# A planned state-space scan on one core: the skip term's matmuls moved to the middle of a half, an urgent copy out of PSUM, and a planner that places TensorE's matmuls one by one

## The chip, the core and the metric

The kernel runs on one core of a Trainium2 chip. The metric is the device time of one execution in microseconds. Before the change the median of three runs is 8321.25 us (8306.08 to 8322.18).

## The reference, cut to what matters

The network has two layers on an image batch `x` of 2 x 96 x 96 x 96. Layer 0 is a convolution block with a selective scan and a small quantized feed-forward net; layer 1 is an attention block with a feed-forward net of the same kind. The change lies in layer 0 (one helper that it touches, the feed-forward net, serves layer 1 too). Of layer 0 this much has to be seen:

```
x_s = grid_sample_bilinear(xin, pos)              # 192 channels, deformed by a learned offset
# the image is cut into 512 sequences of L = 36 pixels; 4 directions k, 192 channels d, 16 states n
x_dbl = einsum('bkdl,kcd->bkcl', xs4, x_proj_weight)      # dts, B, C
delta = softplus(dts @ dt_projs_weight + bias);  A = -exp(A_logs)
for each step t:
    h = h * exp(delta_t * A) + (delta_t * u_t) * B_t      # the scan
    y_t = sum over n of h * C_t
out_y = y + D * u                                          # the skip term
y = sum of the four directions; y = layernorm(y) * silu(z);  out = out_proj(y);  x = x + out
x = x + ffn(layernorm(x))
```

`D * u` is the skip term that the title speaks of. Since the four directions read the same pixels, the kernel adds the four D into one matrix and applies it once.

## The kernel before

Layer 0 works on 32 stripes of 6 image rows (576 pixels, `T`). A stripe has a **front** (`_l0_front`: normalize, project, 3x3 convolution, offsets, bilinear sampling into `xs0` and `xs1`, then B, C, delta and delta*u), a **scan** (`_l0_scan`) and a **back** (`_l0_back`: layer norm over `Y`, gate `zs`, output projection, feed-forward net). Front of stripe n+1, scan of stripe n and back of stripe n-1 run interleaved on the engines.

The scan of a stripe has two **halves** of 96 channels (`h`). Each half accumulates its output in one PSUM bank `y`, of which there is a single buffer. A half has four sections: `o` (row order or column order) times `kk` (forward, backward), each of four quarters of the states, each of two **units** `c` (288 pixels). So a half has 32 units, a stripe 64, and layer 0 has 2048. One unit u is this chain:

- TensorE, `spread` (L1115): B is spread over the partitions, into PSUM `bp` (two buffers, so it needs the scan of unit u-2 to be over);
- VectorE, `product` (L1119): `bp` becomes delta*u*B, then `scan` (L1136): the recurrence, into SBUF `h` (`P.nh` = 6 buffers, so it needs the fold of unit u-6);
- GpSimd, `times_c` (L1141): `h` times C, in place;
- TensorE, `states` (L1153), called the **fold** here: it sums over the states, and adds into `y`.

ScalarE makes the decays `exp(delta*A)` (`dA`, L1099) for two units at a time, two buffers.

At the start of a half, before its first fold, `direct` (L1040, L1042) writes D*u into `y` with six matmuls that also open the accumulation (`start=True`). After the last fold of a half, `out` (L1050, L1052) copies `y` on ScalarE to `Y`; only then can `direct` of the next half begin.

No engine's order is written by hand. All operations of layer 0 go to a planner (`_Plan`). It knows a cost for each operation, made up by hand or from the columns (`_cost`), a due time, the data dependencies and the buffers. `order()` takes in each step the operation that can start earliest; of those that could start at the same time it takes the earliest due. Operations of the scan have due times 60 units early on TensorE and ScalarE (`P.early`), so they win over front and back. An operation marked `first` does more: no other operation of its engine is placed that would end later than `HOLD` after the time at which the marked one can start. Before the change only `spread` is marked, and `out` has an ordinary due time, 33 units after the half's start. An operation may be a group: `run()` then issues several instructions at once, as `direct` does, or the two matmuls that sum over 192 channels in the front and the back.

The planned order is what the engines then follow, each strictly in its order, and each waiting for the data. In time that the plan leaves empty on TensorE, `keep` (L1197) writes matmuls into an unused corner of `y`; it does so only while `P.awake` names a half that is open. A half was opened by `direct`, and is closed by its last fold.

Of the kernel before, what the change touches and what calls it, by code (L numbers as in the profile page):

```python
# [26 lines left out]
C = 96  # L27
# [74 lines left out]
SAME = 0.06  # L102
LAG = {"pe": 0.5, "dve": 1.5, "act": 0.6, "pool": 1.0, "sp": 1.5}
SCAN_LAG = {"pe": 0.2, "dve": 0.3, "act": 0.2, "pool": 0.2, "sp": 1.5}
HOLD = 0.15
SPARE, SHARE, STEP = 0.15, 0.8, 0.15


# [379 lines left out]
def _l0_front(k, P, S, f, x, b, s, at):  # L488
# [157 lines left out]
    def offset(yx, c):  # L646
        po = ps("po")

        def run():
            rest = slice(64 * c, 64 * c + 64)  # L650
            nc.tensor.matmul(po.ap[:, :H2], k.w_off[:, 0, yx], t.ap[:, c], start=True, stop=False)
            nc.tensor.matmul(
                po.ap[:, :H2], k.w_off[rest, 1, yx], t.ap[rest, 2], start=False, stop=True)

        pe(2 * H2, run, ((t, c), (t, 2)), (po,), (fr,))
# [19 lines left out]
    def sample(half):  # L675
        n, X = PART[half], second if half else first
        v = lambda: xin.ap[:n, half, 1:8, 2 : HW + 2]
        fy, fx = lambda: fr.ap[:n, 0], lambda: fr.ap[:n, 1]
        d, tp, bt = (lambda u=u: u.ap[:n, half] for u in (dif, top, bot))
        D, TP, BT = (dif, half), (top, half), (bot, half)  # L680
        pool(672, lambda: tt(d(), xin.ap[:n, half, 1:8, 3 : HW + 3], v(), ALU.subtract), X, (D,))
        pool(T, lambda: tt(tp(), d()[:, 0:6], fx(), ALU.mult), (D, (fr, 1)), (TP,))
        pool(T, lambda: tt(tp(), tp(), v()[:, 0:6], ALU.add), X, (TP,))
        pool(T, lambda: tt(bt(), d()[:, 1:7], fx(), ALU.mult), (D, (fr, 1)), (BT,))
        pool(T, lambda: tt(bt(), bt(), v()[:, 1:7], ALU.add), X, (BT,))
        pool(T, lambda: tt(bt(), bt(), tp(), ALU.subtract), (TP,), (BT,))
        pool(T, lambda: tt(bt(), bt(), fy(), ALU.mult), ((fr, 0),), (BT,))

        def add(c):
            px = ps("px")  # L690
            rows = slice(3 * c, 3 * c + 3)

            def run():
                for j, u in enumerate((tp(), bt())):
                    nc.tensor.matmul(px.ap[:n, :H2], k.ident[:n, :n], u[:, rows, :],
                                     start=(j == 0), stop=(j == 1))

            pe(2 * H2, run, (TP, BT), (px,), (xs0, xs1))
            v = lambda: px.ap[:n, :H2].rearrange("p (i w j) -> p i w j", i=3, w=NW)
            act(H2, lambda: nc.scalar.copy(  # L700
                xs0.ap[:n, half].rearrange("p (w i j) -> p i w j", w=NW, i=WIN)[:, rows], v()),
                (px,), ((xs0, (half, c)),))
            act(H2, lambda: nc.scalar.copy(
                xs1.ap[:n, half].rearrange("p (w j i) -> p i w j", w=NW, j=WIN)[:, rows], v()),
                (px,), ((xs1, (half, c)),))

        for c in range(2):
            add(c)
# [9 lines left out]
    def order_of(o, xs):  # L718
# [4 lines left out]
        for c in range(2):  # L723


            def b_and_c(c=c):
                pb = ps("pb")
                cols = slice(c * H2, (c + 1) * H2)

                def run():  # L730
                    for half in range(2):
                        nc.tensor.matmul(
                            pb.ap[:, :H2],
                            k.w_bc[: PART[half], half, o].rearrange("p j k n -> p (j k n)"),
                            xs.ap[: PART[half], half, cols], start=(half == 0), stop=(half == 1))

                pe(2 * H2, run, (xs,), (pb,), (bt, rest))
# [12 lines left out]

            def deltas(c=c):
                pd = ps("pd")
                cols = slice(c * H2, (c + 1) * H2)

                def run():
                    for half in range(2):
                        nc.tensor.matmul(
                            pd.ap[:C, :H2], k.w_dl[: PART[half], half, o, :],
                            xs.ap[: PART[half], half, cols], start=(half == 0), stop=(half == 1))

                pe(2 * H2, run, (xs,), (pd,), (xd,))
# [112 lines left out]
def _plan_ffn(k, S, op, ps, temp, pool, bufs, ffn, x1, roomy=False):  # L874
# [50 lines left out]
    for c in range(2):  # L925
        def last(c=c):
            py = ps("fpy")

            def run():
                for m in range(NM):  # L930
                    nc.tensor.matmul(py.ap[:C, :H2], ffn.w2[:, m, :], h8.ap[:, m, cols(c)],
                                     start=(m == 0), stop=(m == NM - 1))

            op("pe", 3 * H2 // 2, run, (h8,), (py,), (y16,))
# [9 lines left out]
def _l0_back(k, P, S, f, ffn, res, dst, at):  # L944
# [14 lines left out]
    def both(w, src, name, r):  # L959

        out = ps(name)

        def run():
            for half in range(2):
                nc.tensor.matmul(out.ap[:C, :H2], w(half), src(half),
                                 start=(half == 0), stop=(half == 1))

        op("pe", 2 * H2, run, r, (out,))
        return out

    def centred(c):
# [25 lines left out]
    def project(c):  # L997
# [6 lines left out]
        def run():  # L1004
            nc.tensor.matmul(pp.ap[:C, :H2], k.ident[:C, :C], img(x1), start=True, stop=False)
            for n, (w, v) in enumerate(((k.w_outb, zs), (k.w_out, Y))):
                for h in range(2):
                    nc.tensor.matmul(pp.ap[:C, :H2], w[:, h, :], v.ap[:, h, cols(c)],
                                     start=False, stop=(n == 1 and h == 1))

        op("pe", 5 * H2, run, (Y, zs, (x1, c)), (pp,))
# [12 lines left out]
def _l0_scan(k, P, S, n, f, tau):  # L1024
# [4 lines left out]
    for h in range(2):  # L1029
# [3 lines left out]

        def direct(h=h, py=py):

            P.awake = py
            for b in range(NBL):
                g = NBL * h + b
                w, v = (u[: PART[g // 4]] for u in (k.w_D[:, g], f.xs0.ap[:, g // 4]))
                nc.tensor.matmul(py.ap[b * CB : b * CB + CB, :HEAD], w, v[:, :HEAD],  # L1040
                                 start=True, stop=False)
                nc.tensor.matmul(_tail(py, b), w, v[:, HEAD:], start=b == 0, stop=False)  # L1042

        S.op("pe", 1.4, direct, (f.xs0,), (py,), due=t0)
        for o in range(2):
            for kk in range(2):
                _l0_section(k, P, S, f, 64 * n + 32 * h, o, h, kk, py, t0 + (16 * o + 8 * kk) * tau, tau)

        def out(h=h, py=py):
# [1 line left out]
            for b in range(NBL):  # L1051
                nc.scalar.copy(f.Y.ap[b * CB : b * CB + CB, h, HEAD:], _tail(py, b))  # L1052

        S.op("act", 1.4, out, (py,), (f.Y,), due=t0 + 33 * tau)


HEAD = 14 * SEQ
# [8 lines left out]
def _l0_section(k, P, S, f, first, o, h, kk, py, at, tau):  # L1066
# [42 lines left out]
    def unit(u, i, c, cre, dA, t0):  # L1109
# [35 lines left out]
        S.op("pool", 1.7, times_c, (cre,), (ht,), due=t0 + (2.3 - P.early["pool"]) * tau, scan=True)  # L1145

        def states():
            end = o == 1 and kk == 1 and i == NQ - 1

            def part(dst, v, stop):  # L1150
                if o:
                    v = v.rearrange("p (w j i) -> p w i j", i=WIN, j=WIN)
                nc.tensor.matmul(dst, k.fold, v, start=False, stop=stop)  # L1153

            for blk in range(NBL):
                dst = py.ap[CB * blk : CB * blk + CB]
                n = HEAD - H2 if c else H2
                part(dst[:, c * H2 : c * H2 + n], ht.ap[:, blk, :n], end and c == 1)
            if c:
                for blk in range(NBL):  # L1160
                    part(_tail(py, blk), ht.ap[:, blk, n:], end and blk == NBL - 1)
            P.issued["pe", u] = latest()
            if end and c == 1:
                P.awake = None

        S.op("pe", 0.84, states, (ht,), (py,), due=t0 + (3.5 - P.early["pe"]) * tau, scan=True)

    for i in range(NQ):
        quarter(i)
# [880 lines left out]
```

## Time and profile before

| | us |
|---|---|
| median of three runs | 8321.25 |
| the profiled execution | 8317.46 |
| its span, first to last instruction | 8315.6 |
| layer 0's scans, first to last (146.7 to 6274.0) | 6127.3 |
| VectorE busy in that stretch | 5863.9 |
| TensorE, GpSimd, ScalarE busy in it | 5255.7, 5017.3, 4640.1 |

Busy time of an engine is the time in which at least one of its instructions ran. In the page's groups, each row gives line, engine, operation, tiles and shapes, then busy time, the mean duration of one, and the idle time of that engine just before, with what ended it. A float32 matmul shows as two records. PEld is the loading of weights, which overlaps the matmuls. The lines are those of the kernel before.

### The profile page before, as it was taken

How to read it: one execution, taken by the hardware profiler on the slowest of the kernel's cores; microseconds unless marked ns; L12 is line 12 of the kernel's file. 1: busy time of each engine (PE TensorE's matmuls, PEld its weight loads, DVE VectorE, ACT ScalarE, POOL GpSimd, SP SyncE). 2: the span in 40 equal slices, each digit the busy share in tenths (PEclk: the TensorE clock that was granted, in tenths of full speed). 3: DMA queues.
4: the chain of work that ended last, by engine and by line, in shares of the span. 5: the costliest groups of instructions: out<-in, count | busy, mean ns of one | idle time of the engine just before them, and what ended most of it. 6: DMA issues, size and time to landing. Idle time of an engine off the chain costs nothing. (4 is left out here: it accounts for less than half of the span.)

```text
span 8315.6 us, 123907 instructions
## 1 busy us (share of the span) xinstructions
PE 7287.6 (88%) x46090; PEld 3227.2 (39%) x46090; DVE 7623.0 (92%) x5404; ACT 6253.1 (75%) x10610; POOL 5184.1 (62%) x3835
## 2 busy tenths in 40 slices
PE   7888888888888888888888888888878999989998
PEld 3333333333333344333333333333334223542245
DVE  3999999999999999999999999999996998959988
ACT  5777777777777778787777777777746886678867
POOL 4888878788888888888878888888862000110001
PEclk9999999999999999999999999999999999989999
DMA  3554445444444445444444454544441000110001
GB/s 96 164 161 157 151 152 159 145 156 150 154 156 155 150 155 163 153 155 152 157 148 157 145 162 149 159 153 155 152 139 50 3 2 19 33 46 3 2 23 33
DMA packets 359849, 992.21 MB, mean 119 GB/s; under 512 B 69288, under 2 KB 71680, under 8 KB 359040
## 3 DMA queue, kind: packets, MB, share of 16 engines
q1 hardware_dynamic: 357440, 984.04, 37.7%
q8 instruction: 366, 6.00, 0.3%
q14 instruction: 251, 2.06, 0.1%
q10 hardware_dynamic: 1792, 0.12, 0.0%
HBM read 797.19 MB, written 139.25 MB: 113 GB/s over the span
## 5 line engine op out<-in xcount | busy, mean ns | idle before, releaser
L1141 POOL TENSOR_TENSOR h<-h,cre 128x864 f32<-128x864 f32 x2048 | 3486.0, 1714 | 1024.8 <-DVE h L1136 632.0
L1136 DVE TENSOR_TENSOR_SCAN h<-dA,bp 128x864 f32<-128x864 f32 x2048 | 3887.1, 1935 | 157.5 <-PE y L1153 145.9
L1099 ACT ACTIVATE dA<-dlr,A 128x576 f32<-128x576 f32 x3072 | 2156.9, 765 | 1019.6 <-DVE h L1136 914.7
L1119 DVE TENSOR_TENSOR bp<-dur,bp 128x864 f32<-128x864 f32 x2048 | 2062.7, 1045 | 155.3 <-DMA dur<-du_d 46.8
L1153 PE MATMUL y<-h,fold 128*32 128x288 f32 (+2 forms) x18432 | 1776.9, 437 | 103.4 <-POOL h L1141 98.5
L1115 PE MATMUL bp<-bt,selb 128*128 128x288 bf16 x2048 | 619.3, 302 | 690.1 <-DVE h L1136 679.2
L1512 ACT ACTIVATE pr<-sc 128x960 f32<-128x960 f32 (+1 forms) x1080 | 954.1, 937 | 199.7 <-PE sc L1508 178.3
L1153 PEld LDWEIGHTS y<-h,fold 128*32 128x32 f32 x18432 | 726.2, 114 | 746.3 <-POOL h L1141 396.3
L1592 DVE TENSOR_TENSOR sums<-sums,pr 128x3840 f32<-128x3840 f32 (+1 forms) x240 | 959.0, 3996 | 55.6 <-ACT pr L1512 33.1
L1684 POOL MEMSET vch<- 96x32 f32 x16 | 2.5, 154 | 1299.8 <-DVE dist L1546 1207.9
L1115 PEld LDWEIGHTS <-selb 128*128 128x128 bf16 x2048 | 197.4, 96 | 1348.3 <-DVE h L1136 1231.7
L1508 PE MATMUL sc<-qH,kH 32*128 32x480 f32 (+1 forms) x3240 | 627.0, 602 | 9.8 <-DMA q<-qH 5.3
L1197 PE MATMUL y<-selb,minus 128*32 128x288 bf16 x3205 | 598.1, 298 | 0.0
L1508 PE MATMUL sc<-q,kH 32*128 32x480 f32 (+1 forms) x1080 | 564.4, 602 | 0.0
L1574 PE MATMUL av<-pr,vT 128*32 128x480 f32 (+1 forms) x4320 | 533.0, 564 | 3.7 <-ACT av L1599 3.5
L1765 DVE SCALAR_TENSOR_TENSOR acc<-vch,lepe_w,acc 96x1152 f32<-96x1152 f32 x320 | 470.0, 1469 | 8.2 <-ACT vch L1700 0.4
L1508 PEld LDWEIGHTS sc<-qH,kH 32*128 32x128 f32 x3240 | 219.1, 184 | 418.8 <-issue 218.1
L1197 PEld LDWEIGHTS <-minus 128*32 128x32 bf16 x3205 | 272.4, 98 | 263.8 <-issue 192.3
L617 PE MATMUL pc<-xin,w_ca 128*128 128x288 f32 x1152 | 368.5, 423 | 0.1
L940 POOL TENSOR_TENSOR x<-x,fy 96x576 f32<-96x576 f32 x32 | 52.0, 1626 | 477.5 <-ACT fy L939 401.1
L797 PE MATMUL pt<-xd,w_dt 96*128 96x288 f32 x768 | 281.5, 454 | 4.3 <-ACT r L803 1.1
L816 POOL TENSOR_TENSOR e<-e,du 128x576 f32<-128x576 f32 x192 | 231.5, 1206 | 43.7 <-ACT du L812 43.6
(284 smaller groups left out, 10914.1 us busy)
## 6 DMA issues: line engine op xcount, KB each, us to landing
cre<-c_d SPq DMA_DIRECT2D x1024, 288.0 KB, 3.3
dur<-du_d SPq DMA_DIRECT2D x256, 864.0 KB, 5.5
dlr<-dl_d SPq DMA_DIRECT2D x256, 864.0 KB, 5.1
x<-xs SPq DMA_DIRECT2D x512, 72.0 KB, 2.8
du_d<-du SPq DMA_DIRECT2D x128, 288.0 KB, 2.9
dl_d<-dl SPq DMA_DIRECT2D x128, 288.0 KB, 4.0
du_d<-du SPq DMA_DIRECT2D x128, 144.0 KB, 2.5
dl_d<-dl SPq DMA_DIRECT2D x128, 144.0 KB, 3.0
```

The costliest lines, as they stand in the source:

```text
L1099: nc.scalar.activation(dA.ap[:, :, blk, :], dlr.ap[:, blk, :].rearrange("p (c n) -> p c n", c=2), AF.Exp, scale=k.A[:, i, kg, h, blk : blk ...
L1115: nc.tensor.matmul(bp.ap[:, :H2], k.selb[:, kk, i, :], f.bc[o].ap[:, toks], start=True, stop=True)
L1119: nc.vector.tensor_tensor(bp.ap[:, : NBL * H2].rearrange("p (b n) -> p b n", b=NBL)[:, ::-1], dur.ap[:, ::-1, toks], bp.ap[:, :H2].unsquee ...
L1136: nc.vector.tensor_tensor_scan(hv, dv, bv, 0.0, ALU.mult, ALU.add)
L1141: nc.gpsimd.tensor_tensor(ht.ap, ht.ap, cre.ap[:, toks].unsqueeze(1).to_broadcast([128, NBL, H2]), ALU.mult)
L1153: nc.tensor.matmul(dst, k.fold, v, start=False, stop=stop)
L1197: nc.tensor.matmul(P.awake.ap[NBL * CB :, T - HEAD + 2 * 72 : HEAD], k.minus[:, :CB], k.selb[:, 0].rearrange("p i m -> p (i m)")[:, : HEAD ...
L1508: nc.tensor.matmul(two[to // 2][:, to % 2, :n], kH[rows, k0 : k0 + 128], q, start=True, stop=True)
L1512: nc.scalar.activation(pr[:, 2 * i : 2 * i + 2, :n], two[i][:, :, :n], AF.Exp, scale=HD**-0.5)
L1574: nc.tensor.matmul((main if s < HEADS else other)[s * HD : (s + 1) * HD, :n], vT[:, blk, hd, :], pr[:, place(s, p), :n], start=at == 0, st ...
L1592: nc.vector.tensor_tensor(both, both, pr[:, :, :, :n], ALU.add)
L1765: S.op("dve", 1.43, lambda: nc.vector.scalar_tensor_tensor(acc.ap, src(), W.lw[:, t : t + 1], acc.ap, ALU.mult, ALU.add), (vch,), (acc,))
```

## The change

It has five parts.

1. `direct` moves from the start of a half to the start of the section o = 1, kk = 0 (unit 16 of 32), with its due time. It no longer opens the accumulation; the first folds of a half do (`start=True` for unit 0's and, for the tail columns, unit 1's).
2. `out` becomes an operation of the scan with a due time 60 units before the half's start, where it was 33 units after it.
3. `states` is marked `first`, as `spread` is; `HOLD` goes from 0.15 to 0.4.
4. Groups of matmuls in front, back and feed-forward net become single operations of the plan. What they compute, and in which order within a group, stays.
5. `P.awake` is set by the fold of unit 1 instead of by `direct`.

```
-HOLD = 0.15
+HOLD = 0.4
...
-            def run():
-                for j, u in enumerate((tp(), bt())):
-                    nc.tensor.matmul(px.ap[:n, :H2], k.ident[:n, :n], u[:, rows, :],
-                                     start=(j == 0), stop=(j == 1))
-
-            pe(2 * H2, run, (TP, BT), (px,), (xs0, xs1))
+            for j, u in enumerate((tp, bt)):
+                pe(H2, lambda j=j, u=u: nc.tensor.matmul(
+                    px.ap[:n, :H2], k.ident[:n, :n], u()[:, rows, :],
+                    start=(j == 0), stop=(j == 1)), (TP, BT), (px,), (xs0, xs1))
```

The same is done to the groups of `offset` (2 matmuls), `b_and_c` (2), `deltas` (2), `last` in the feed-forward net (3), `both` (2) and `project` in the back (5). Then, in `_l0_scan` and `_l0_section`:

```
         def direct(h=h, py=py):
 
-            P.awake = py
             for b in range(NBL):
                 ...
                 nc.tensor.matmul(py.ap[b * CB : b * CB + CB, :HEAD], w, v[:, :HEAD],
-                                 start=True, stop=False)
-                nc.tensor.matmul(_tail(py, b), w, v[:, HEAD:], start=b == 0, stop=False)
-
-        S.op("pe", 1.4, direct, (f.xs0,), (py,), due=t0)
+                                 start=False, stop=False)
+                nc.tensor.matmul(_tail(py, b), w, v[:, HEAD:], start=False, stop=False)
+
         for o in range(2):
             for kk in range(2):
+                if o and not kk:
+                    S.op("pe", 1.4, direct, (f.xs0,), (py,), due=t0 + 16 * tau)
                 _l0_section(...)
...
-        S.op("act", 1.4, out, (py,), (f.Y,), due=t0 + 33 * tau)
+        S.op("act", 1.4, out, (py,), (f.Y,), due=t0 - P.early["act"] * tau, scan=True)
...
         def states():
+            new = o == 0 and kk == 0 and i == 0
             end = o == 1 and kk == 1 and i == NQ - 1
             ...
-                part(dst[:, c * H2 : c * H2 + n], ht.ap[:, blk, :n], end and c == 1)
+                part(dst[:, c * H2 : c * H2 + n], ht.ap[:, blk, :n], end and c == 1, new and c == 0)
             ...
-            if end and c == 1:
-                P.awake = None
-
-        S.op("pe", 0.84, states, (ht,), (py,), due=t0 + (3.5 - P.early["pe"]) * tau, scan=True)
+            if c and (new or end):
+                P.awake = None if end else py
+
+        S.op("pe", 0.84, states, (ht,), (py,), due=t0 + (3.5 - P.early["pe"]) * tau,
+             scan=True, first=True)
```

More of the change, by code (lines that the diff above doesn't have):

```diff
@@ L647, in offset @@
         po = ps("po")
-        def run():
[L650 to L655, printed above, removed]
+        rest = slice(64 * c, 64 * c + 64)
+        pe(H2, lambda: nc.tensor.matmul(
+            po.ap[:, :H2], k.w_off[:, 0, yx], t.ap[:, c], start=True, stop=False),
+            ((t, c), (t, 2)), (po,), (fr,))
+        pe(H2, lambda: nc.tensor.matmul(
+            po.ap[:, :H2], k.w_off[rest, 1, yx], t.ap[rest, 2], start=False, stop=True),
+            ((t, 2),), (po,), (fr,))
         def share():
@@ L691, in add @@
             rows = slice(3 * c, 3 * c + 3)
-            def run():
-                for j, u in enumerate((tp(), bt())):
-                    nc.tensor.matmul(px.ap[:n, :H2], k.ident[:n, :n], u[:, rows, :],
-                                     start=(j == 0), stop=(j == 1))
-            pe(2 * H2, run, (TP, BT), (px,), (xs0, xs1))
+            for j, u in enumerate((tp, bt)):
+                pe(H2, lambda j=j, u=u: nc.tensor.matmul(
+                    px.ap[:n, :H2], k.ident[:n, :n], u()[:, rows, :],
+                    start=(j == 0), stop=(j == 1)), (TP, BT), (px,), (xs0, xs1))
             v = lambda: px.ap[:n, :H2].rearrange("p (i w j) -> p i w j", i=3, w=NW)
@@ L728, in b_and_c @@
                 cols = slice(c * H2, (c + 1) * H2)
[L730 to L737, printed above, removed]
+                for half in range(2):
+                    pe(H2, lambda half=half: nc.tensor.matmul(
+                        pb.ap[:, :H2],
+                        k.w_bc[: PART[half], half, o].rearrange("p j k n -> p (j k n)"),
+                        xs.ap[: PART[half], half, cols], start=(half == 0), stop=(half == 1)),
+                        (xs,), (pb,), (bt, rest))
                 def split():
@@ L753, in deltas @@
                 cols = slice(c * H2, (c + 1) * H2)
[L755 to L761, printed above, removed]
+                for half in range(2):
+                    pe(H2, lambda half=half: nc.tensor.matmul(
+                        pd.ap[:C, :H2], k.w_dl[: PART[half], half, o, :],
+                        xs.ap[: PART[half], half, cols], start=(half == 0), stop=(half == 1)),
+                        (xs,), (pd,), (xd,))
                 act(H2, lambda: nc.scalar.copy(xd.ap[:, cols], pd.ap[:C, :H2]), (pd,), ((xd, c),))
@@ L927, in last @@
             py = ps("fpy")
[L929 to L934, printed above, removed]
+            for m in range(NM):
+                op("pe", H2 // 2, lambda m=m: nc.tensor.matmul(
+                    py.ap[:C, :H2], ffn.w2[:, m, :], h8.ap[:, m, cols(c)],
+                    start=(m == 0), stop=(m == NM - 1)), (h8,), (py,), (y16,))
             op("act", H2, lambda: nc.scalar.copy(y16.ap[:, cols(c)], py.ap[:C, :H2]),
@@ L961, in both @@
         out = ps(name)
[L963 to L968, printed above, removed]
+        for half in range(2):
+            op("pe", H2, lambda half=half: nc.tensor.matmul(
+                out.ap[:C, :H2], w(half), src(half), start=(half == 0), stop=(half == 1)),
+                r, (out,))
         return out
@@ L1002, in project @@
             "p i (w j) -> p w i j", j=WIN)
[L1004 to L1011, printed above, removed]
+        op("pe", H2, lambda: nc.tensor.matmul(
+            pp.ap[:C, :H2], k.ident[:C, :C], img(x1), start=True, stop=False), (Y, zs, (x1, c)), (pp,))
+        for n, (w, v) in enumerate(((k.w_outb, zs), (k.w_out, Y))):
+            for h in range(2):
+                op("pe", H2, lambda n=n, w=w, v=v, h=h: nc.tensor.matmul(
+                    pp.ap[:C, :H2], w[:, h, :], v.ap[:, h, cols(c)],
+                    start=False, stop=(n == 1 and h == 1)), (v,), (pp,))
         op("act", H2, lambda: nc.scalar.copy(
@@ L1147, in states, with part @@
         def states():
+            new = o == 0 and kk == 0 and i == 0
             end = o == 1 and kk == 1 and i == NQ - 1
-            def part(dst, v, stop):
+            def part(dst, v, stop, start):
                 if o:
                     v = v.rearrange("p (w j i) -> p w i j", i=WIN, j=WIN)
-                nc.tensor.matmul(dst, k.fold, v, start=False, stop=stop)
+                nc.tensor.matmul(dst, k.fold, v, start=start, stop=stop)
             for blk in range(NBL):
@@ L1157, in states @@
                 n = HEAD - H2 if c else H2
-                part(dst[:, c * H2 : c * H2 + n], ht.ap[:, blk, :n], end and c == 1)
+                part(dst[:, c * H2 : c * H2 + n], ht.ap[:, blk, :n], end and c == 1, new and c == 0)
             if c:
                 for blk in range(NBL):
-                    part(_tail(py, blk), ht.ap[:, blk, n:], end and blk == NBL - 1)
+                    part(_tail(py, blk), ht.ap[:, blk, n:], end and blk == NBL - 1, new and blk == 0)
             P.issued["pe", u] = latest()
-            if end and c == 1:
-                P.awake = None
-        S.op("pe", 0.84, states, (ht,), (py,), due=t0 + (3.5 - P.early["pe"]) * tau, scan=True)
+            if c and (new or end):
+                P.awake = None if end else py
+        S.op("pe", 0.84, states, (ht,), (py,), due=t0 + (3.5 - P.early["pe"]) * tau,
+             scan=True, first=True)
     for i in range(NQ):
```

## Prediction, made before the changed kernel was run

> **What bounds the kernel now.** I read the busy time of layer 0's stretch first (the table by windows), then who VectorE waits for in it, then the timeline of each engine around the longest wait. From the windows:
>
> ```profile
> 146.70:6274.00 6127.30, 5255.73 (x33729) 2389.65 (x33728) 5863.89 (x4278) 4640.07 (x8079) 5017.30 (x3606) 0.95 0.48 153
> ```
>
> Columns are the length, then busy time of TensorE, its weight loads, VectorE, ScalarE, GpSimd. VectorE is busy 5863.9 of 6127.3 us; 263.4 us are idle. Two groups of the page make nearly all of its work, and GpSimd's largest shows the next resource:
>
> ```profile
> L1141 POOL TENSOR_TENSOR h<-h,cre 128x864 f32<-128x864 f32 x2048 | 3486.0, 1714 | 1024.8 <-DVE h L1136 632.0
> L1136 DVE TENSOR_TENSOR_SCAN h<-dA,bp 128x864 f32<-128x864 f32 x2048 | 3887.1, 1935 | 157.5 <-PE y L1153 145.9
> L1119 DVE TENSOR_TENSOR bp<-dur,bp 128x864 f32<-128x864 f32 x2048 | 2062.7, 1045 | 155.3 <-DMA dur<-du_d 46.8
> ```
>
> Per unit VectorE needs 3887.1/2048 = 1.90 us for the scan and 2062.7/2048 = 1.01 for the product. The change touches neither, so it can win or lose only idle time: at most 263 us here. The waits of VectorE in that stretch (us in all, times, longest):
>
> ```profile
> DVE h L1136 <- PE y L1153: 145.9, 46, 9.8
> DVE bp L1119 <- PE bp L1115: 32.8, 52, 1.4
> DVE bp L1119 <- PE y L1153: 30.3, 23, 1.6
> ```
>
> The first is the scan waiting for a fold, that is for one of the six `h` buffers. Counting scans up to each of its 46 waits: 16 stand before the same scan, that of unit 6 of the second half of a stripe, and hold 121.3 us. Thirteen of these last 8.1 to 9.8 us. One, on VectorE, TensorE and ScalarE:
>
> ```profile
> 821.77 1.06 DVE L1119 TENSOR_TENSOR bp<-dur,bp 128x864 f32<-128x864 f32 x1
> 831.93 3.80 DVE L1136 TENSOR_TENSOR_SCAN h<-dA,bp 128x864 f32<-128x864 f32 x2 [9.10 <-PE y L1153]
> ```
>
> ```profile
> 821.43 0.30 PE L1115 MATMUL bp<-bt,selb 128*128 128x288 bf16 x1 [0.44 <-DVE h L1136]
> 821.57 1.15 PE L579 MATMUL pz<-xn,in_proj 96*96 96x288 f32 x4
> 825.62 1.21 PE L579 MATMUL pz<-xn,in_proj 96*96 96x288 f32 x4 [2.90 <-ACT zs L582]
> 827.05 1.05 PE L1040 MATMUL y<-xs,w_D 128*32 128x504 f32 x1 [0.22 <-ACT Y L1052]
> ...
> 829.71 1.06 PE L1040 MATMUL y<-xs,w_D 64*32 64x504 f32 x2
> 830.70 1.54 PE L1153 MATMUL y<-h,fold 128*32 128x288 f32 x15
> ```
>
> ```profile
> 823.86 1.28 ACT L582 ACT_TABLE_LOAD   x1
> 825.15 0.71 ACT L582 ACTIVATE zs<-pz 96x288 f32<-96x288 f32 x2
> 825.75 0.57 ACT L1050 COPY Y<-y 96x504 f32<-96x504 f32 x1
> 826.34 0.66 ACT L1052 COPY Y<-y 32x72 f32<-32x72 f32 x3
> ```
>
> The chain: `out` stands on ScalarE behind a table load and two gates; `direct` stands on TensorE behind two `pz` matmuls that need those gates; the first fold of the new half stands behind `direct`, which takes 3.7 us here (827.05 to 830.77). VectorE has filled all six buffers and waits.
>
> **The skill.** *TensorE: Matmul & The Clock Gate*, "Step-by-step: what each phase is for": "The MATMULs themselves stay in program order". The trace agrees: a fold with its data ready waits 2.90 us behind a `pz`. The same page, "What's actually happening": after an idle window of about 3.4 us the array runs at half clock. `direct` takes 1.06 to 2.0 us at the boundaries that don't stall and 3.0 to 3.7 at the thirteen that do; the gap before it is 2.90 us, a little under that window, so the clock may be why, but this trace doesn't prove it. *ScalarE: Activation LUTs*, "What ACT_TABLE_LOAD costs": about 1283 ns a load; the trace has 1283 for each.
>
> **The change, part by part.** I compared the built order of both kernels, instruction by instruction on each engine; it holds no times.
>
> *Moving `direct`, urgent `out` (parts 1, 2).* At 13 boundaries of the old order `out` stands behind the decays of units u+8, and the first fold behind the spread of u+7, four `pz` and `direct`: the thirteen long waits. In the new order this is left at one boundary of 63 (stripe 4). Elsewhere `out` stands behind the decays of u+2 or u+4, eight times of u+6. The start of scan u+6 lies 15.3 us (median of the trace) after the end of scan u. Decays of u+4 can start when scan u+1 is over, 2.9 us into that; then at most 2.5 us of other work, decays 2.1, `out` 1.23, fold 0.7: done by 9.5 of 15.3. With u+6: start at 8.7, then 2.1 + 1.8 + 1.23 + 0.7 = 14.5, still inside. So **-121.3 us, +8.7** for the one left (a mean long wait). Between 0 and 130 is possible.
>
> *`direct` in the middle.* Its six matmuls now stand behind the spread of unit 17 to 22, with one to four folds behind them, since all folds from unit 16 on write the same `y`. Worst case, behind the spread of unit 22: spread 0.3 + direct 2.0 + fold 0.7 = 3.0 us, while VectorE has a scan (1.9) and two products (2.0) before it needs unit 16's buffer. The last fold of such a pile delays the next spread; the new order has the product of the other unit 5.8 us later there. Taken 0; if `direct` took the cold 3.7, 1 us a half, 64 us.
>
> *Folds `first`, `HOLD`, single matmuls (3, 4).* A fold standing behind the spread of unit u+6 or u+7 is one that leaves VectorE hardly any time. There are 161 + 59 = 220 in the old order and 83 + 34 = 117 in the new, 47% fewer. The waits for folds outside the boundary are 145.9 - 121.3 + 30.3 = 54.9 us; 47% of that is **-26 us** (0 to -55). HOLD 0.4 lets another matmul run 0.25 longer past the moment a spread is due. The second product of a pair has about 0.5 us to spare (first product 1.0, less the spread's 0.3 and the hand-over), so most of that is hidden; I add **+10 us** to the 32.8 (bounds 0 and 250, see the rivals).
>
> *GpSimd.* Nothing is added, but the order moves. Front and back put runs of tensor operations of 1.21 us between two `times_c`. Runs of twelve or more: 14 in the old order (all of twelve), 30 in the new (20 of twelve, 10 of thirteen). A run of twelve (14.5 to 14.9) with `times_c` before and after (2 x 1.7) and a fold with its hand-over (0.9) ends 19.2 us after scan u; the buffer of u+1 is needed at 2.9 + 15.3 = 18.2. That is 1.0 us each, and 2.3 for thirteen. Old 14 x 1.0, new 20 x 1.0 + 10 x 2.3 = 43: **+29 us** (0 to 112, the latter 3.5 us in each of 32 stripes).
>
> *ScalarE.* The gates are planned in more pieces: 22 more loads of their table and 22 back, 44 x 1.283 = 56 us. Cover: ScalarE is busy 4640 of 6127, and decays may come 5.6 us late (two scans and four products, 7.7, less their 2.1) while a load, a gate and a load back take 3.0. Taken 0 (0 to +56).
>
> *The rest.* `keep` goes from 3205 to 3528 matmuls, 323 x 0.14 us in gaps of TensorE's plan: 0, hidden as TensorE is busy 86%. DMAs: as many as before, SP's order shifts with the plan; waits for `dur` were one, at the start: 0. In layer 1 the feed-forward's three last matmuls are planned singly; SP and GpSimd keep their order there, the others shift locally: 0, +-8.
>
> Sum: -121.3 + 8.7 - 26 + 10 + 29 = -99.6 us. The profiled execution took 8317.5 us by its own time, 0.05% under the median of 8321.25, so I need no correction: 8317.5 - 99.6 = **8218 us**.
>
> **Rivals.** *GpSimd takes it back* (0.2): the stall gave GpSimd its time to catch up; without it the runs cost 1.8 to 3.5 us in every stripe, 58 to 112 instead of 29: 8247 to 8300, I take 8280. For it: GpSimd's lag already grows to 15 us behind the scan at unit 7. Against: it is busy 82% and idle 2.6 us at the long wait.
> *Spreads come late* (0.09), which ends slower: were HOLD's 0.25 us not hidden, each of the 1010 pairs of products would pay it: +250, 8317.5 - 121 + 9 - 26 + 29 + 250 = 8458. It decides once spreads end over 0.6 us after the scan that frees them. Against: a 288-column float32 matmul takes 0.48 us back to back where the planner charges 0.58, so the real engine runs ahead of its plan; and VectorE waited for a spread only 52 times in 2048.
> *The wait changes its name* (0.06): `out` is still late, since ScalarE's order changes little in time or table loads come ahead of it: 8317.
> The forecast has 0.65.
>
> **Numbers.** A measurement of this kernel can tell about 0.2% (17 us) from no change. The forecast's own range, with 0 to -55 for folds and half the bounds of the others, is 8160 to 8270; the GpSimd case reaches to 8300. Range 8150 to 8300. Faster by over 0.2%: 0.84 (forecast and nearly all of the GpSimd case), within: 0.07, slower: 0.09.
>
> **What would show it.** After: the wait of the scan (L1125) for `y` L1143 drops from 145.9 to below 50 us, no wait of 8 us but one; VectorE's idle time in layer 0 is near 165 us; D's matmuls take 1 to 2 us. GpSimd's case shows as scans of units 9 to 14 waiting for folds that waited for L1130; late spreads as `bp` L1108 waiting for L1104 with far over 33 us. I am wrong if long waits at the boundary are gone and the time isn't.

## The result, and the profile after

The changed kernel takes 8276.36 us (median of five, 8270.01 to 8282.34) against 8321.25 (8304.28 to 8322.18). The ratio of the means is 0.9954, with a 95% interval from 0.994 to 0.9969. It is faster, by 45 us by the medians and 38 by the means, where 103 were forecast. The profiled execution took 8276.3 us, 41.2 less than the one before.

The table by windows for the new layer 0, from the start of its first scan to the end of its last (length, then busy TensorE, weight loads, VectorE, ScalarE, GpSimd, then the granted clock):

```profile
149.40:6226.90 6077.50, 5297.01 (x34106) 2420.16 (x34105) 5896.18 (x4278) 4695.24 (x8118) 5018.97 (x3605) 0.96 0.49 154
```

VectorE's idle time is 181.3 us, but its busy time has grown by 32.3. The same three groups of the page:

```profile
L1130 POOL TENSOR_TENSOR h<-h,cre 128x864 f32<-128x864 f32 x2048 | 3475.2, 1713 | 957.4 <-DVE h L1125 639.7
L1125 DVE TENSOR_TENSOR_SCAN h<-dA,bp 128x864 f32<-128x864 f32 x2048 | 3900.6, 1939 | 51.2 <-PE y L1143 30.6
...
L1108 DVE TENSOR_TENSOR bp<-dur,bp 128x864 f32<-128x864 f32 x2048 | 2082.2, 1048 | 187.9 <-PE bp L1104 81.4
```

The scan's idle time fell from 157.5 to 51.2 us; the product's rose from 155.3 to 187.9, and its main releaser is now the spread. VectorE's waits in that stretch (us in all, times, longest):

```profile
DVE bp L1108 <- PE bp L1104: 81.4, 106, 2.6
DVE h L1125 <- PE y L1143: 30.6, 26, 4.7
DVE bp L1108 <- POOL h L1130: 27.8, 40, 1.9
```

Scans waited for folds for 145.9 us and now do for 30.6. Products waited for spreads for 32.8 and now do for 81.4.

For all comparisons I measured each kernel from the start of its first scan to the end of its last (before: 146.7 to 6269.9), and sorted VectorE's waits of 0.15 us or more by what ended them. "Boundary" is the scan of unit 6 of a half waiting for a fold. "Just behind `times_c`" is a wait for a fold that ended at most 1.3 us after its own `times_c`, so that GpSimd and not TensorE's queue held it up; the other folds waited for ended 1.8 us or more after theirs.

| us | before | after | difference | forecast |
|---|---|---|---|---|
| stretch | 6123.2 | 6077.6 | -45.6 | -99.6 |
| VectorE busy | 5863.9 | 5896.3 | +32.4 | 0 |
| boundary waits (number) | 121.4 (16) | 4.7 (1) | -116.7 | -112.6 |
| other waits for folds | 54.8 | 28.7 | -26.1 | -26 |
| of these, just behind `times_c` | 9.1 | 23.1 | +14.0 | |
| waits for `times_c` | 17.0 | 28.3 | +11.3 | +29 |
| waits for spreads (number) | 32.8 (52) | 81.4 (106) | +48.6 | +10 |
| all other idle time | 33.3 | 38.2 | +4.9 | 0 |

Around the stretch, the start came 2.7 us later and layer 1 took 1.9 us more. So three questions stand: why VectorE is busier, why spreads come late, and which part of the change ended the boundary waits.

### The profile page after: what moved, and what is told of

It is laid out like the page before. It is cut to its first block, busy times and chain, and to the rows that moved or that the text cites. A ratio compares the mean times of both kernels' runs of the same rounds, so it can differ in the third digit from the quotient of the medians.

```text
span 8274.5 us, 124621 instructions
## 1 busy us (share of the span) xinstructions
PE 7337.5 (89%) x46413; PEld 3261.5 (39%) x46413; DVE 7653.1 (92%) x5404; ACT 6308.6 (76%) x10654; POOL 5188.3 (63%) x3835
## 5 line engine op out<-in xcount | busy, mean ns | idle before, releaser
L1125 DVE TENSOR_TENSOR_SCAN h<-dA,bp 128x864 f32<-128x864 f32 x2048 | 3900.6, 1939 | 51.2 <-PE y L1143 30.6
L1108 DVE TENSOR_TENSOR bp<-dur,bp 128x864 f32<-128x864 f32 x2048 | 2082.2, 1048 | 187.9 <-PE bp L1104 81.4
L1188 PEld LDWEIGHTS <-minus 128*32 128x32 bf16 x3528 | 298.0, 98 | 225.6 <-issue 131.2
L810 POOL TENSOR_TENSOR e<-e,du 128x576 f32<-128x576 f32 x192 | 231.1, 1204 | 60.0 <-ACT du L806 59.7
```

What stands on the lines that cost most here:

```text
L1108: nc.vector.tensor_tensor(bp.ap[:, : NBL * H2].rearrange("p (b n) -> p b n", b=NBL)[:, ::-1], dur.ap[:, ::-1, toks], bp.ap[:, :H2].unsquee ...
L1125: nc.vector.tensor_tensor_scan(hv, dv, bv, 0.0, ALU.mult, ALU.add)
L1188: nc.tensor.matmul(P.awake.ap[NBL * CB :, T - HEAD + 2 * 72 : HEAD], k.minus[:, :CB], k.selb[:, 0].rearrange("p i m -> p (i m)")[:, : HEAD ...
```

## The experiments

Each kernel was timed beside the kernel before. In the table, the columns from "busy" on are microseconds in the stretch of the profiled execution: VectorE's busy and idle time, its boundary waits, its waits for spreads, and the time in which the trace gives TensorE's clock as 0.5 ("half clock"). "Pairs" is the edit of E4.

| kernel | us | ratio (95%) | busy | idle | boundary | spread | half clock |
|---|---|---|---|---|---|---|---|
| before | 8321.25 | | 5863.9 | 259.3 | 121.4 | 32.8 | 597 |
| after | 8276.36 | 0.9954 (0.994-0.9969) | 5896.3 | 181.3 | 4.7 | 81.4 | 430 |
| E1 parts 1, 2, 5 | 8267.99 | 0.9942 (0.9929-0.9954) | 5866.1 | 201.4 | 40.3 | 40.0 | 290 |
| E2 part 4 | 8262.2 | 0.994 (0.9927-0.9953) | 5873.0 | 197.2 | 44.1 | 52.3 | 570 |
| E3 part 3 | 8240.15 | 0.9914 (0.9899-0.9929) | 5882.2 | 171.4 | 82.6 | 58.3 | 365 |
| E4 after + pairs | 8199.41 | 0.9859 (0.9845-0.9873) | 5861.2 | 132.2 | 0 | 127.2 | 304 |
| E5 before + pairs | 8096.92 | 0.9737 (0.9724-0.975) | 5852.7 | 48.1 | 0 | 13.5 | 116 |
| E6 E5, HOLD 0.4 | 8154.82 | 0.9804 (0.9791-0.9818) | 5858.3 | 105.6 | 0 | 95.7 | 375 |
| E7 all dependent | 8497.3 | 1.0219 (1.0204-1.0235) | 6061.0 | 230.9 | 79.3* | 31.4 | 341 |
| E8 after, HOLD 0.15 | 8466.02 | 1.018 (1.0166-1.0194) | 5877.4 | 402.8 | 237.8 | 78.5 | 911 |
| E9 before, D's cost | 8284.07 | 0.9954 (0.9939-0.9969) | 5870.0 | 231.1 | 71.7 | 63.6 | 700 |
| E10 after, HOLD 0.41 | 8359.03 | 1.0053 (1.0037-1.007) | 5895.0 | 242.0 | 101.6 | 21.2 | 99 |
| E11 E4, folds not first | 8197.76 | 0.9847 (0.983-0.9864) | 5867.2 | 139.8 | 0 | 60.9 | 440 |
| E12 E1 + pairs | 8184.36 | 0.983 (0.9815-0.9846) | 5862.5 | 129.9 | 0 | 102.0 | 403 |
| E13 after, more keep | 8244.32 | 0.99 (0.9882-0.9918) | 5894.4 | 156.7 | 5.6 | 53.0 | 270 |
| E14 after, no keep | 8415.74 | 1.0106 (1.0085-1.0127) | 5909.4 | 317.1 | 4.7 | 165.7 | 1896 |
| E15 E6, more keep | 8107.33 | 0.9741 (0.9723-0.9758) | 5857.7 | 56.2 | 0 | 46.3 | 181 |
| E16 E12, more keep | 8172.03 | 0.9815 (0.9796-0.9835) | 5859.6 | 106.0 | 0 | 57.2 | 232 |
| E17 E5, more keep | 8095.57 | 0.9726 (0.971-0.9742) | 5852.4 | 46.4 | 0 | 15.4 | 72 |

*In E7 product and scan are issued as one, and this wait shows at the product of unit 6 instead of its scan: 25 waits, twelve of them of 6.0 us.

### The parts alone: E1, E2, E3

E1 is the kernel before with `direct` in the middle, `out` urgent and `P.awake` set by the fold. E2 is the kernel before with part 4's single matmuls. E3 is this:

```
-HOLD = 0.15
+HOLD = 0.4
...
-        S.op("pe", 0.84, states, ..., scan=True)
+        S.op("pe", 0.84, states, ..., scan=True, first=True)
```

> The kernel before with parts 1, 2 and 5 alone: D in the middle of a half, the copy of y urgent; HOLD stays 0.15, folds are not first, groups stay groups. In its built order no product stands directly before its own scan on VectorE, 213 folds stand behind the spread of u+6 or u+7 (220 before), the copy stands behind the decays of u+8 at 10 boundaries (13 before), and GpSimd has 25 runs of twelve or thirteen operations. Theory (the gain is the end of the chain copy, D, fold; the loss of the whole change comes from late spreads and from products directly before their scans, which parts 3 and 4 bring): a boundary wait is left at those 10 but without D's 3.7 us, some 5 us each, so -121 + 50; spread waits stay near 33 us; GpSimd's runs +25: about 8270. Rival (the place of the copy alone decides, D is nothing): 10 x 9 us stay, 8310.

> The kernel before with part 4 alone: single matmuls in the plan; D opens the half as before, the copy has its old due time, HOLD 0.15. In its built order the copy stands behind the decays of u+8 at one boundary of 63 only, 162 folds stand behind the spread of u+6 or u+7, no product stands directly before its own scan. Theory that the thirteen waits are an accident of the planned order (any part that reshuffles it ends them): -121 + 9, folds -15, spread waits near 33: about 8195, faster than the whole change. Rival (D and the copy must be moved to end the waits): 8310 to 8320.

> The kernel before with part 3 alone: folds first, HOLD 0.4. Its built order has 188 products directly before their own scan, 56 folds behind the spread of u+6 or u+7, the copy behind the decays of u+8 at 10 boundaries with D behind it. Theory (part 3 brings late spreads and dependent pairs): spread waits near 80 us (+48), 188 pairs at 0.125 us +24, folds -25, boundary waits 10 x 9 instead of 121: about 8335. Rival (part 3 only helps, late spreads come from single matmuls): spread waits stay near 33 and the time is 8260 to 8280.

E1 came out as forecast; E2, forecast at 8195, and E3, at 8335, did not. Each part alone is as good as all together or better: 0.9942, 0.994 and 0.9914 against 0.9954. If gains added up, the three would give 2.0%; together they give 0.46%. E1 has 15 boundary waits left, nine of 3.5 to 7.3 us, so moving D and urging the copy does not end them by itself. E2, which moves neither, cuts them from 121.4 to 44.1 us. VectorE's busy time grows by 2.2 us in E1, 9.1 in E2 and 18.3 in E3: most of the extra busy time comes with part 3, some with part 4.

### VectorE's busy time: E4, E7

In VectorE's built order of the kernel before, no scan stands directly behind its own product; P(u), P(u+1), S(u), S(u+1) is the usual run. In the order after, 233 scans do; in E3's, 188. E4 forbids it, with one more dependency in the planner ("pairs"): the scan of an even unit comes after the product of the odd one.

```
-        S.op("dve", 0.96, product, ...)
-        S.op("dve", 1.87, scan, ...)
+        prod = S.op("dve", 0.96, product, ...)
+        sc = S.op("dve", 1.87, scan, ...)
+        if c:
+            P.even.deps.add(prod)
+        P.even = sc
```

E7 does the opposite to the kernel after: product and scan are one operation of the plan, so that all scans follow their own product.

```
+        def both():
+            product()
+            scan()
+        S.op("dve", 2.83, both, (dur, dA), (bp, ht), due=t0 - P.early["dve"] * tau, scan=True)
```

> The changed kernel with one line more in the plan: the scan of an even unit depends on the product of the odd unit after it, so products and scans come in pairs. In its built order no product stands directly before its own scan (233 in the changed kernel), 5 folds stand behind the spread of u+6 or u+7 (117), GpSimd has one run of twelve (30), the copy never stands later than behind the decays of u+4. Theory (a product directly before its own scan loses the overlap of two instructions, 0.125 us): VectorE's busy time falls by 29 us, waits for folds go to near 5 us (-25), spread waits stay near 80: about 8220. Rival (the pairs only turn the loss into waits for the odd unit's spread): busy time falls and spread waits grow by as much, 8265 to 8280.

> The changed kernel with product and scan of a unit as one operation of the plan, so that all 2048 products (233 in the changed kernel) stand directly before their own scans. The next spread has a whole product and scan, 2.9 us, to be done. Theory (a product directly before its own scan costs the overlap of two neighbours, 0.125 us): VectorE's busy time falls by little or none while its gaps under 0.15 us and lost overlaps add 1815 x 0.125 = 227 us, spread waits go to under 10 us (-75), boundary waits come back at 12 places (+50): about 8475. Rival (it costs nothing; the busy time of the changed kernel rose for another reason): about 8250.

E7 on VectorE's timeline (start, duration, instruction):

```profile
2999.43 1.04 DVE L1108 TENSOR_TENSOR bp<-dur,bp 128x864 f32<-128x864 f32 x1
3000.51 1.95 DVE L1124 TENSOR_TENSOR_SCAN h<-dA,bp 128x864 f32<-128x864 f32 x1
3002.38 1.04 DVE L1108 TENSOR_TENSOR bp<-dur,bp 128x864 f32<-128x864 f32 x1
```

The product ends at 3000.47 and its scan starts at 3000.51: a gap. That scan ends at 3002.46, but the next product, which doesn't need it, has started at 3002.38: an overlap of 80 ns. A unit takes 2.95 us. With pairs, on the timeline of E5 (below), both changes overlap:

```profile
3002.08 3.79 DVE L1136 TENSOR_TENSOR_SCAN h<-dA,bp 128x864 f32<-128x864 f32 x2
3005.78 2.00 DVE L1119 TENSOR_TENSOR bp<-dur,bp 128x864 f32<-128x864 f32 x2
3007.69 1.95 DVE L1136 TENSOR_TENSOR_SCAN h<-dA,bp 128x864 f32<-128x864 f32 x1
```

Two units take 3007.69 - 3002.08 = 5.61 us, 2.81 each. Over E7, against E4, the price of one dependent pair is (6061.0 - 5861.2 + 75.3)/2047 = 0.134 us, where 75.3 is the sum of E7's gaps under 0.15 us, nearly all of them the 34 ns behind a product (1.1 in E4). For the 233 pairs of the change that makes an estimated 31 us: 8.6 of gaps (idle time) and about 23 of the 32.4 of busy time. Lost overlap by itself is 19.1 us there (the sum of all durations less the busy time falls from 342.1 to 323.0); the other 13.3 are longer durations, of which only a part is the pairs': E2, without a dependent pair, has 9.6 us of them, and their cause is open. E4, with none, takes 77 us less than the kernel after; its stretch is 84 us shorter, 35 of it busy time and 49 idle. Pairs also leave no boundary wait and 3.0 us of waits for folds; but spreads come late for 127.2 us. E7's boundary waits came back at the twelve places forecast.

### The pairs without the change: E5, E6

E5 is the kernel before with the pairs alone. E6 is E5 with HOLD 0.4 instead of 0.15.

> The kernel before, with none of the change, and the line that makes products and scans come in pairs (the scan of an even unit depends on the product of the odd one). HOLD 0.15. Its built order has no product directly before its own scan, as before, but the plan comes out otherwise: the copy never stands later than behind the decays of u+4 (13 times behind u+8 before), 64 folds stand behind the spread of u+6 or u+7 (220), GpSimd has one run of twelve (14). Theory (the thirteen waits are an accident of the plan; late spreads come with HOLD 0.4): no boundary waits though D opens the half and the copy isn't urgent, folds 10, spreads 35 to 50: idle near 75 us instead of 259, 8130 to 8145. Rival (spread waits show as soon as the other waits go, whatever HOLD is): spread waits over 100 us, 8190 to 8210.

> As the kernel before with pairs, and HOLD 0.4 instead of 0.15; folds are not first, groups stay groups. In its built order 3 folds stand behind the spread of u+6 or u+7, the copy stands behind the decays of u+2 but for one boundary. Nothing but spreads is left to wait for. Theory (HOLD is what makes spreads late): spread waits 80 to 130 us against those of the kernel with HOLD 0.15, time 8190. Rival (folds marked first make spreads late): spread waits as with HOLD 0.15, time 8130.

E5's waits of VectorE in layer 0:

```profile
DVE bp L1119 <- issue: 19.0, 27, 0.8
...
DVE bp L1119 <- PE bp L1115: 13.5, 39, 1.2
```

The first row ("issue") is time for which the profile shows no release. Nothing waits long: idle time is 48.1 us of 5900.9, and the kernel takes 8096.92 us, 2.6% less than before, with `direct` at the start of a half, `out` due late and grouped matmuls. So none of the parts 1 to 5 is needed to end the boundary waits. The old order had no dependent pairs, so the 224 us aren't their price: the constraint leads the planner to another order in which `out`, folds and spreads come in time. Why it does wasn't settled. E6 shows what HOLD does to that kernel, with the new order that it brings: waits for spreads rise from 13.5 to 95.7 us, 84.0 of it while TensorE is at half clock, and the time by 58 us.

### How firm the order is: E8, E9, E10

If the boundary waits belong to the place of D and of the copy, small changes of the planner's numbers should not bring them back. E8 is the kernel after with HOLD 0.15, E10 the same with 0.41 (0.4 is in the change). E9 is the kernel before with this alone:

```
-        S.op("pe", 1.4, direct, (f.xs0,), (py,), due=t0)
+        S.op("pe", 1.45, direct, (f.xs0,), (py,), due=t0)
```

> The changed kernel with HOLD back at 0.15. Its built order has 48 products directly before their scans (233), but the copy stands behind the decays of u+8 at 27 boundaries (1), and 167 folds stand behind the spread of u+6 or u+7 (117). Theory: spread waits fall from 81 to near 40 us, dependent pairs give 23 us back, boundary waits (without D behind the copy) take 27 x 3 us and folds 20 more: about 8300. Rival (spread waits don't hang on HOLD): they stay near 80, time 8340.

> The kernel before with one number changed: the planner's cost of D at the start of a half, 1.45 instead of 1.4. Nothing that runs is another instruction; the plan comes out otherwise. In its built order the copy stands behind the decays of u+8 at 4 boundaries (13 before), 205 folds stand behind the spread of u+6 or u+7 (220). Theory (whether the copy comes before or after the decays of u+8 is an accident of the plan, and that alone makes the long waits): 4 long waits of 9 us in place of 13, -85: about 8235. Rival (the waits belong to D at the start of a half): 8300 to 8320.

> The changed kernel with HOLD 0.41 instead of 0.40. In its built order the copy stands behind the decays of u+8 at 26 boundaries (1 in the changed kernel), 269 products stand directly before their scans (233), GpSimd has 27 runs of thirteen (10). Theory (order by accident): 26 boundary waits of some 6 us, +156, dependent pairs +5, GpSimd +30: about 8465. Rival (0.01 of HOLD is nothing): 8276.

E8's waits, and ScalarE's timeline up to the copy at one boundary:

```profile
DVE h L1125 <- PE y L1143: 271.9, 58, 11.5
DVE bp L1108 <- PE bp L1104: 78.5, 89, 2.4
```

```profile
1616.23 0.39 ACT L744 CAST bt<-pb 32x288 bf16<-32x288 f32 x1 [1.31 <-PE pb L741]
1617.44 0.57 ACT L1039 COPY Y<-y 96x504 f32<-96x504 f32 x1 [0.81 <-PE pp L998]
```

With D in the middle and an urgent copy, 27 boundaries wait for 237.8 us in all. At this one the copy stands behind casts for B that wait for matmuls, and TensorE is at half clock from 1604 to 1618 and busy without a gap for the last 8 us of that; D has no part in it. Of the 237.8 us, 229.8 lie at half clock. E10, with HOLD higher by 0.01, has 26 boundary waits of some 4 us, nearly all at full clock, and is slower than the kernel before. And E9, whose one cost differs by 0.05 us, takes 71.7 instead of 121.4 us at the boundaries and comes to a ratio of 0.9954, the same as the whole change. I had forecast 8300, 8235 and 8465 us; the runs gave 8466.02, 8284.07 and 8359.03. I could not forecast the time of an order from the edit, and a gain of 45 us is no larger than what a nudge of one number gives.

### Late spreads, and HOLD: E11, E12

E11 is E4 without `first=True` on `states`. E12 is E1 with the pairs, HOLD 0.15.

> The changed kernel with pairs, folds not first, HOLD still 0.4. Against the kernel with pairs whose folds are first. Its built order has 126 folds behind the spread of u+6 or u+7 (5), the copy behind the decays of u+6 at 14 boundaries (none). Theory (folds first put 97 us of spread waits behind folds; HOLD alone makes the rest): spread waits with a fold ahead fall under 10 us, spread waits from other matmuls 40 to 90 us, fold and boundary waits 50: 8180 to 8220. Rival (late spreads come from HOLD alone): waits behind folds stay near 97.

> Parts 1, 2 and 5 (D in the middle, urgent copy) with pairs, at HOLD 0.15, folds not first, groups kept: the kernel before with pairs, plus the move. Its built order has 108 folds behind the spread of u+6 or u+7 (64 without the move), the copy behind the decays of u+2 or u+4 but for one. Theory (the move is worth nothing once the plan has the copy early): spread waits under 40 us, fold waits 30: 8110 to 8140, not faster than 8097. Rival (the move helps in itself): 8060 to 8085.

In E4 a fold stood ahead of the late spread in 97.0 of 127.2 us; in E11 this is 8.3 of 60.9. So urgent folds do push spreads back, but waits for folds come back (3.0 to 30.9 us), as do those for `times_c` (0.3 to 23.0), and the time is the same. E12 is E5 with parts 1, 2 and 5, and takes 87 us more, which neither its theory nor its rival had: with the pairs in place the move loses. It also refutes the simple account of HOLD: with 0.15 it has 102.0 us of late spreads, while E10 with 0.41 has 21.2 (in its shortest execution, that of the profile). What E12 shares with E6 is the clock: 77.2 of its 102.0 us lie in stretches at half clock.

### The clock: E13, E14, E15, E16, E17

At one late spread of the kernel after, first on VectorE, then on TensorE's timeline:

```profile
3404.97 1.95 DVE L1125 TENSOR_TENSOR_SCAN h<-dA,bp 128x864 f32<-128x864 f32 x1
3407.63 1.06 DVE L1108 TENSOR_TENSOR bp<-dur,bp 128x864 f32<-128x864 f32 x1 [0.71 <-PE bp L1104]
3411.25 1.06 DVE L1108 TENSOR_TENSOR bp<-dur,bp 128x864 f32<-128x864 f32 x1 [2.56 <-PE bp L1104]
```

```profile
3407.05 0.45 PE L1104 MATMUL bp<-bt,selb 128*128 128x288 bf16 x1
3407.29 1.17 PE L956 MATMUL yc<-Y,minus_mean 96*96 96x288 f32 x2
3408.25 1.17 PE L956 MATMUL yc<-Y,less_mean 96*96 96x288 f32 x2
3409.34 0.42 PE L1188 MATMUL y<-selb,minus 128*32 128x288 bf16 x1
3409.70 1.28 PE L956 MATMUL yc<-Y,less_mean 96*96 96x288 f32 x2
3410.76 0.45 PE L1104 MATMUL bp<-bt,selb 128*128 128x288 bf16 x1
```

Four operations stand between two spreads and fill 3.7 us without a gap. The two records of one float32 matmul take 1.17 us here; at full clock they take 0.65 us (L998 at 1018.56, below). The windows of the same place, before the drop and after it (the clock is the third column from the right):

```profile
3394.70:3398.20 3.50, 2.25 (x21) 0.88 (x21) 3.50 (x3) 2.40 (x4) 3.50 (x3) 1.00 0.60 240
3404.00:3411.50 7.50, 7.50 (x17) 3.65 (x18) 4.20 (x4) 4.91 (x10) 6.50 (x7) 0.50 0.07 28
```

From 3398.23 to 3415.30 the clock is 0.5. TensorE then has no idle time left, and VectorE is busy for 4.20 of 7.50 us. To test that the clock is the cause and not a sign of it, E13 and E14 leave the order as it is and change only how many `keep` matmuls are written into TensorE's gaps: 4634 in E13 and none in E14, where the change has 3528.

```
-SPARE, SHARE, STEP = 0.15, 0.8, 0.15
+SPARE, SHARE, STEP = 0.15, 1.0, 0.15
```

E14 has 0.0 there. E15, E16 and E17 are E6, E12 and E5 with 1.0.

> The changed kernel with SHARE 1.0 instead of 0.8: 4634 keep matmuls for 3528. The plan and the order of everything else are the same. In the changed kernel's trace TensorE's clock is at half for 430 us of the scans' stretch, and 59 of the 81 us of spread waits fall there. Theory (spreads are late because TensorE's matmuls take twice as long at half clock): half clock under 250 us, spread waits near 50 us, about 8245. Rival (HOLD and folds first make spreads late, the clock only goes with it, and keep matmuls stand in the way): 8276 to 8300.

> The changed kernel with SHARE 0: no keep matmuls, the plan and the order of everything else the same. Theory (half clock): half clock well over 1000 us, spread waits over 150 us, folds later too, over 8350. Rival (keep matmuls are in the way): spread waits under 81 us, at or below 8276.

> The kernel before with pairs and HOLD 0.4, with SHARE 1.0: 4919 keep matmuls for 3792, the plan the same. With SHARE 0.8 it had 375 us of half clock, and 85 of its 96 us of spread waits fell there, against 116 us and 14 us with HOLD 0.15. Theory (half clock, not HOLD): half clock under 200 us, spread waits under 55 us, 8115 instead of 8155. Rival (HOLD): 96 us of spread waits stay.

> The move of D and the copy with pairs at HOLD 0.15, with SHARE 1.0. With 0.8 it had 102 us of spread waits, 80 of them with a keep matmul as the last thing ahead of the spread, 79 of them at half clock (403 us in all). Theory (half clock): spread waits under 65 us, 8150 instead of 8184. Rival (keep matmuls delay the spreads): waits grow past 102 us, 8190 to 8210.

> The kernel before with pairs (HOLD 0.15, no part of the change) and SHARE 1.0. With SHARE 0.8 it took 8097 us, with 48 us of VectorE's idle time left in the scans, 14 of it for spreads. Half-clock theory: half clock 116 us to some 60, at most 10 us to gain: 8085 to 8097. Rival (with so little waiting left, more keep matmuls only get in the way): 8100 to 8115.

The waits for spreads, in E13, then in E14:

```profile
DVE bp L1108 <- PE bp L1104: 53.0, 78, 2.5
```

```profile
DVE bp L1108 <- PE bp L1104: 165.7, 201, 3.1
```

And the granted clock in 40 slices of the span, after, then E14:

```profile
PEclk8999998999999999999999999999999999989999
```

```profile
PEclk7888888888988889888989888898767999989999
```

With the same plan, half clock lasts 1896, 430 and 270 us for 0, 3528 and 4634 such matmuls, late spreads 165.7, 81.4 and 53.0, and the times are 8415.74, 8276.36 and 8244.32. So with one and the same order the clock sets most of how late spreads come. Executions of one kernel agree with it: E10's four took 8330.81 us at a mean granted clock of 0.98 and 8352.06 to 8374.23 at 0.970 to 0.973. With more such matmuls E15 gets back 47 us of E6's 58 (spreads 95.7 to 46.3). E16 gains only 12: spreads fall by 45 us, but waits for `times_c` rise from 10 to 30. E17, which had little at half clock to begin with, stays within its scatter of E5. E17 and E5 are the best versions: 8095.57 and 8096.92 us, 2.2% under the changed kernel.

But the clock alone isn't what set the new kernel apart from the old. The kernel before has more half clock, 597 us against 430, and fewer late spreads; 18.9 of its 32.8 us of such waits lie at half clock, and 52.7 of the 81.4 after. The new order meets half clock with more late spreads, and no run shows which part of it does that.

## Why the prediction was right or wrong

- **The boundary waits: right in size, wrong in cause.** One of 63 is left, in stripe 4 as read from the order, with 4.7 us instead of 8.7. On TensorE's timeline the gate of the back and the last projection still stand ahead of that fold:

```profile
1018.56 0.65 PE L998 MATMUL pp<-zs,w_outb 96*96 96x288 f32 x2
...
1023.60 0.73 PE L579 MATMUL pz<-xn,in_proj 96*96 96x288 f32 x2 [1.00 <-ACT zs L582]
1024.82 1.90 PE L1143 MATMUL y<-h,fold 128*32 128x288 f32 x36 [0.50 <-ACT Y L1041]
```

  The bracket names the copy (L1041) as what released the fold. But E1 keeps 15 such waits with both parts in it, and E5 has none without them. The built order gave the right number; that the moving of D and the urgent copy bring it about was wrong.
- **Other folds, -26 us: right in the number only.** Measured -26.1, but two changes cancel. Waits for folds that TensorE's queue held up fell from 45.7 to 5.6 us, -40.1, more than the counting of folds behind the spreads of units u+6 and u+7 gave. Waits for folds just behind their `times_c` rose by 14.0; these belong to GpSimd.
- **"The change touches neither, so it can win or lose only idle time": the first step that failed.** Busy time grew by 32.4 us. The durations of a scan and a product moved little (1935 to 1939 and 1045 to 1048 ns, 13.3 us in all); their neighbours moved more. The built order showed in advance that 233 scans stood right behind their own product, and none before. I had compared the orders, but drew nothing from VectorE's for its busy time, and no trace of before shows what such a pair costs.
- **Spreads, +10 us: the second.** Measured +48.6. The bounds (0 and 250) held it. I had priced HOLD's 0.25 us as hidden and asked whether TensorE runs ahead of its plan; it does at full clock, but not at half. Of the 81.4 us, 52.7 lie at half clock. Spreads that end over 0.6 us after the scan that frees them, the mark that the prediction set for its rival "Spreads come late", went from 336 to 604 of 2048, so that rival was at work in a part of the units. That HOLD alone sets them falls (E10, E12); that the clock sets how late they come in a given order is shown (E13, E14); why the new order has more of them than the old, at less half clock, stays open.
- **GpSimd, +29: near right.** VectorE's waits for `times_c` grew by 11.3 us, and those for folds just behind their `times_c` by 14.0: 25.3 in all, from 26.1 to 51.4. The second kind stands, all but 0.4 us, at units 10 to 15 of a half, near the 9 to 14 named in advance. One, after a run of thirteen on GpSimd, waits 2.05 us where 2.3 was the price; on GpSimd, TensorE and VectorE:

```profile
2272.31 1.21 POOL L682 TENSOR_TENSOR top<-dif,fr 128x576 f32<-128x576 f32 x1
...
2288.31 5.05 POOL L1130 TENSOR_TENSOR h<-h,cre 128x864 f32<-128x864 f32 x3
```

```profile
2290.07 0.69 PE L1143 MATMUL y<-h,fold 128*32 128x288 f32 x6 [1.01 <-POOL h L1130]
```

```profile
2290.88 3.80 DVE L1125 TENSOR_TENSOR_SCAN h<-dA,bp 128x864 f32<-128x864 f32 x2 [2.05 <-PE y L1143]
```

- **D in the middle and layer 1: right at 0; ScalarE's table loads: nearly.** D's blocks take 1.06 to 2.01 us. The prediction left open why they took 3.0 to 3.7 at the thirteen long waits: the trace has them there at half clock for 72 to 100% of their time. ScalarE has the 44 more loads, and VectorE's waits for it grew by 6.1 us, from 13.3 to 19.4. Layer 1 changed by 1.9 us.

The forecast missed the stretch by 54.0 us: 32.4 busy, 38.6 spreads, 4.9 others, less 14.1 of folds in TensorE's queue, 3.7 of GpSimd and 4.1 of the boundary. The direction and the range held.

Open: why the pairs lead to so good an order in either kernel; why E10's order has boundary waits that the change's has not, 0.01 us of HOLD apart; why the new order has more late spreads than the old; what sets the length of a boundary wait (0.3 to 11.5 us). The clock is a part of that last one in some orders (80.6 of the 121.4 us before, 229.8 of E8's 237.8), but E3 and E10 have 82.6 and 101.6 us of such waits nearly all at full clock. For the last three, no run takes one cause alone away.

## What to carry to other kernels

When a planner writes the order, an edit's gain is that of a whole new order: compare the built orders on the bounding engine first, down to which instruction stands right behind which, and try a nudge of one planner number (E9) before crediting the edit. What looked like a scheduling problem was in part a clock problem: matmuls with no result to give, in gaps already there, moved this kernel by 171 us (E13 against E14). One constraint on the order of neighbours that the planner doesn't price (E5) did more here than urging single operations, though why its order is so good isn't shown.

## What was not expected of the hardware

- **Neighbours on VectorE overlap if they are independent.** The next instruction starts 80 to 90 ns before the one ahead ends; a scan behind its own product starts 34 ns after it. Dependent pairs cost 0.134 us each, with the scan's mean at 1954 ns in E7 against 1937 in E4.
- **TensorE's clock halved without an idle window.** The Trainium skill, *TensorE: Matmul & The Clock Gate*, "What's actually happening", puts half clock after at least one idle window of about 3.4 us. Here the 3.5 us ahead of a drop hold 2.25 us of work (window 3394.70 above) and no gap over 1.1 us; ahead of the spells at half clock in the changed kernel's stretch (56, of 3.4 to 20.5 us) TensorE was busy for about 53% of the last 3.5 us. So a half-filled window was enough here, though some matmul records can be missing.
- **It stays at half clock while it is full.** The same section puts full clock after one busy window of about 3.4 us. From 3398.23 to 3415.30 TensorE shows as busy for all of 17.07 us, and the clock (third from the right) stayed at 0.5:

```profile
3398.23:3415.30 17.07, 17.07 (x51) 7.91 (x44) 13.13 (x10) 11.27 (x24) 15.75 (x14) 0.50 0.37 114
```
